# The queries of two attentions, made one batch earlier at two crossings between layers

## The chip, the cores and the metric

The kernel runs on one core of one Trainium2 chip. The metric is the device time of one execution in microseconds; the time given for a version is the median of its runs. "PE" is the engine for matrix products, "DVE", "ACT" and "POOL" are the vector, scalar and GpSimd engines, and "SP" is the engine whose queue issues most DMAs. Each engine works through its own queue in order.

## The reference

A decoder of four layers works on `x`, 8 batches of 256 tokens with 128 channels, and a context of 8 batches of 512 tokens. Each layer has a self-attention, a cross attention or the like, and a feed-forward part; each part reads a layer norm of `x` and is added to `x`:

```python
x = x + _L2_attn_ref(_layernorm(x, axis=-1), ...)            # sparse causal ("fenwick") attention
x = x + _L2_xattn_ref(_layernorm(x, axis=-1), ctx_1024, ...) # cross attention, 16 heads of 8
x = x + _L2_ffn_ref(_layernorm(x, axis=-1), ...)             # gate and up products, quantised to 8 bits
x = x + _L3_attn_ref(_layernorm(x, axis=-1), ...)            # causal attention, 16 heads of 8
```

Batches do not mix in the attentions. The L2 feed-forward part takes one maximum over all tokens for its quantisation scale, twice.

## The kernel before

`x` stays in on-chip memory as 16 tiles of 128 tokens, and `xt` holds the transposed layer norm of each batch, on which products work. A batch is "normed" once `_norm` (statistics on DVE, the power on POOL, `ln_z` on DVE) and `_normed` (two transposes on PE into `ln_ps`, one copy by ACT into `xt`) have run for it.

Work is written as Python generators that yield between steps, so that the steps of one layer can be put among those of the next. The framework turns the program into one instruction queue for each engine and may move an instruction ahead of others that it does not depend on; the products of the attentions are pinned to program order by `_Heads.mm` and `_Heads.turn_over`.

The attentions with 16 heads of 8 (the cross attention of layer 2 and the causal attention of layer 3 among them) share `_Heads`. For each batch, `steps(b)` makes keys, queries and values:

- `project("k", ...)` and `project("q", ...)`: one product on PE into `mh_kps` or `mh_qps`, an evacuation with bias by ACT into `mh_kf` or `mh_qf` (L426), and a split into two parts by POOL into `mh_kp` or `mh_qp` (L428 and L429);
- `spread_k` and `spread_q`: four and eight DMAs issued by SP (L434 and L439), which lay the heads out into `mh_k` and `mh_q`;
- `values`: products into `mh_vps`, copied by ACT into `mh_v`;
- `rest`: a row added to `x` by POOL (`pre_add`, the lines `x<-x,mh_row`).

`first()` does this for batch 0 in two halves with one yield between them: first keys, part of the spreading and the values, and then queries, `pre_add` and the rest of the spreading. Afterwards `_heads_attention` computes `mh_sps` (scores for the row maximum), and with a lag the exponentials and outputs. Its generator argument `guest` is work of the layer before it, for later batches, which goes on among the steps of the attention.

There are two crossings that matter here.

**From the sparse attention to the cross attention of layer 2**, in `_middle`. `fa(0, 1)` is the sparse attention of batches 0 and 1. It goes through half-batches `t` = 0 to 3 with `weigh` (products `fa_kvps` of shifted inputs, evacuated by DVE at L1115 and by ACT at L1118, then softmax, then weighted values on POOL at L1137 and L1139) and `apply` (`fa_o`, `fa_tps`, `fa_ot`, `fa_yps`, and at odd `t` the layer norm), and yields the number of a batch when that batch is normed. Before it runs, `next(begun)` has made the keys and values of batch 0. After it has run to its end, `next(begun, None)` makes the queries.

**From the feed-forward part of layer 2 to the causal attention of layer 3**, in `_l2_ffn`. `pair(0, ...)` takes the down products of batches 0 and 1 (`qf_hq`, `qf_dps`, `qf_y`), adds them to `x`, and then norms batch 0 and batch 1, with a yield of the batch number after each. When it is done, `E.draining()` runs the whole `beginning` of the causal attention: keys, values and queries of batch 0.

In the lines of the profile, L460 is the helper `_Heads.mm`, L463 is `_Heads.transpose`, and L215 is the copy into `xt`.

Of the kernel before, what the change touches and what calls it, by code (L numbers as in the profile page):

```python
# [187 lines left out]
def _norm(E, b, engine=None):  # L188

    nc = E.nc  # L190
    st = E.ln.tile([P, 2, 6], F32, name="ln_st")
    mv = E.ln.tile([P, 2, 2], F32, name="ln_mv")
    for q in range(2):
        nc.vector.bn_stats(st[:, q, :], E.x[:, 2 * b + q, :])
        nc.vector.bn_aggr(mv[:, q, :], st[:, q, :])  # L195
    rstd = E.ln.tile([P, 2], F32, name="ln_rstd")
    nc.gpsimd.tensor_scalar(rstd, mv[:, :, 1], EPS, None, ALU.add)  # L197
    nc.gpsimd.tensor_tensor(rstd, rstd, E.neg_half[:, :2], ALU.pow)  # L198
    z = E.ln.tile([P, 2, D], F32, name="ln_z")
    for q in range(2):  # L200
        (engine or nc.vector).tensor_scalar(  # L201
            z[:, q, :], E.x[:, 2 * b + q, :], mv[:, q, 0:1], rstd[:, q : q + 1], ALU.subtract, ALU.mult
        )
    return z


def _normed(E, b, z, psum, turn_over=None):

    ps = psum.tile([P, 2, D], F32, tag="g", name="ln_ps")
    for q in range(2):  # L210
        if turn_over:
            turn_over(ps[:, q, :], z[:, q, :])
        else:
            E.nc.tensor.transpose(ps[:, q, :], z[:, q, :], E.ident)
    E.nc.scalar.copy(E.xt(b), ps.rearrange("p q t -> p (q t)"))  # L215
# [6 lines left out]
def _run(steps):  # L222
    for _ in steps:
        pass
# [955 lines left out]
def plain_pe(E):  # L1180

    E.mm, E.transpose = E.nc.tensor.matmul, E.nc.tensor.transpose
    E.turn_over = lambda out, in_: E.nc.tensor.transpose(out, in_, E.ident)


def _middle(E, names, then):

    nc = E.nc  # L1190
    plain_pe(E)
    banks = lambda to, name, bufs, side="left": to.enter_context(
        E.tc.tile_pool(name=name, bufs=bufs, space=PSUM, side=side)
    )
    if names != MIDDLE:
        for n in names:
            with ExitStack() as scope:
                pg = E.mid_ln = banks(scope, "mid_pg", 6)
                E.banks = SimpleNamespace(fa=pg, rk=pg, ln=pg)
                unit = {  # L1200
                    "L0_ffn": _l0_ffn, "L1_attn": _l1_attn, "L1_xattn": _l1_xattn, "L1_ffn": _l1_ffn,
                    "L2_attn": _l2_attn,
                }[n](E, scope, *([pg] if n in MIDDLE[:3] else []))
                if n == "L2_attn":
                    _run(unit(0, 4))
                    continue
                for g in range(4):
                    _run(unit(g) or ())
        E.close_weights()
        return  # L1210
    last, psum, scope, early = (ExitStack() for _ in range(4))
    E.mid_ln = banks(psum, "mid_ln", 1)
    mid = banks(scope, "mid_pg", 4, "right")
    moe = _l0_ffn(E, scope, banks(early, "moe_pg", 3))
    ra, xa = _l1_attn(E, scope, mid), _l1_xattn(E, scope, mid)
    rk = _l1_ffn(E, scope, "right")
    E.banks = SimpleNamespace(rk=mid, ln=E.mid_ln)
    for s in range(4):
        if s > 2:
            _run(rk(s - 3))  # L1220
        if s > 1:
            xa(s - 2)
        if s:
            ra(s - 1)
        moe(s)
    early.close()
    E.close_big()
    ra(3)
    xa(2)
    xa(3)  # L1230
    scope.close()
    E.banks.fa = banks(psum, "fa_pg", 3)
    fa = _l2_attn(E, last)
    guest = then in HEADS
    begun = E.beginning(then)
    if guest:
        next(begun)
    _run(fa(0, 1))
    if guest:
        next(begun, None)  # L1240
    psum.close()

    def rest():
        if guest:
            g = E.heads.g
            E.mm, E.turn_over, E.transpose = E.heads.mm, E.heads.turn_over, E.heads.transpose
            E.banks = SimpleNamespace(fa=g, rk=g, ln=g)
        with ExitStack() as own:
            if not guest:
                g = banks(own, "mid_pg2", 6)  # L1250
                E.banks = SimpleNamespace(fa=g, rk=g, ln=g)
            yield from fa(1, 3, _l1_ffn(E, own))
        last.close()
        E.close_weights()
        if guest:
            yield from _l2_ffn_weights(E, E.heads.g)

    E.guest = rest()
    if not guest:
        _run(E.guest)  # L1260
# [5 lines left out]
def _quantise(E, pool, to, of, inv):  # L1266

    n, w = to.shape[0], to.shape[1]
    u = pool.tile([P, 512], F32, name="qf_t")[:n, :w]
    E.nc.vector.tensor_scalar(u, of, inv, 127.0, ALU.mult, ALU.min)  # L1270
    E.nc.vector.tensor_scalar(u, u, -128.0, ROUND, ALU.max, ALU.add)
    E.nc.scalar.activation(to, u, AF.Identity, bias=E.unround[:n, :])
# [53 lines left out]
def _l2_ffn(E, ctx):  # L1326
# [11 lines left out]
    wk = ctx.enter_context(E.tc.tile_pool(name="qf", bufs=2))  # L1338
    pg = ctx.enter_context(E.tc.tile_pool(name="qf_pg", bufs=6, space=PSUM))
# [47 lines left out]
    def pair(g, pool, bank):  # L1387

        hq = pool.tile([P, 3, 512], BF16, name="qf_hq")
        for c, n in QUARTERS:  # L1390
            _quantise(E, pool, hq[:n, c, :], h[:n, c, g, :], inv_h[:n, :])
            yield
        ps = bank.tile([P, 4, D], F32, tag="g", name="qf_dps")
        for t in range(4):
            for c, n in QUARTERS:
                E.mm(ps[:, t, :], hq[:n, c, t * P : t * P + P], f.down[:n, c, :], start=c == 0, stop=c == 2)
        y = pool.tile([P, 4, D], F32, name="qf_y")
        nc.vector.tensor_tensor(y, ps, f.row.unsqueeze(1).to_broadcast([P, 4, D]), ALU.mult)
        yield
        zs = []  # L1400
        for b in range(2):
            E.add(2 * g + b, y[:, 2 * b : 2 * b + 2, :])
            zs.append(_norm(E, 2 * g + b))
        for _ in range(3):
            yield
        for b in range(2):
            _normed(E, 2 * g + b, zs[b], bank, E.turn_over)
            yield 2 * g + b

    guest = E.following in HEADS  # L1410
    for g in range(1 if guest else 4):
        _run(pair(g, wk, pg))
    E.draining()

    def rest():
        E.mm, E.turn_over, E.transpose = E.heads.mm, E.heads.turn_over, E.heads.transpose
# [12 lines left out]
def _l3_ffn(E, ctx):  # L1429
# [103 lines left out]
}  # L1533
LAYERS = {
    "L2_xattn": _l2_xattn, "L2_ffn": _l2_ffn,
    "L3_attn": _l3_attn, "L3_xattn": _l3_xattn, "L3_ffn": _l3_ffn,
}
# [4 lines left out]
def kernel(ctx: ExitStack, tc: tile.TileContext, ins, at, out, layers=ALL):  # L1542
    nc = tc.nc
    const = ctx.enter_context(tc.tile_pool(name="const", bufs=1))
    E = SimpleNamespace(nc=nc, tc=tc, ins=ins)
# [88 lines left out]
    begun = set()  # L1634

    def heads():

        E.heads = _Heads(E, hd)
        E.unfilled = list(E.heads.fills())
# [3 lines left out]
    def beginning(layer):  # L1643

        if layer in HEADS and layer not in begun:
            begun.add(layer)
            if not E.heads:
                heads()
            fills, E.unfilled = E.unfilled, []
            for f in fills[:4]:  # L1650
                f()
            HEADS[layer](E)
            yield from E.heads.first()
            for f in fills[4:]:
                f()

    def begin(layer):

        for _ in beginning(layer):
            pass  # L1660
# [62 lines left out]
    for i, part in enumerate(parts):  # L1723
# [13 lines left out]
        if kind(layer) == "middle":  # L1737
            hd.close()
            E.heads = None
            prefetch(then)  # L1740
            _middle(E, part, following)
            continue
# [34 lines left out]
```

## Time and profile before

| | us |
|---|---|
| median of 3 runs | 1782.96 (1779.84 to 1785.97) |
| profiled execution, its time | 1784.95 |
| profiled execution, its span | 1783.2 |
| PE busy | 1471.9 (83%) |
| DVE busy | 1149.2 (64%) |
| ACT busy | 881.3 (49%) |
| POOL busy | 495.7 (28%) |
| mean granted PE clock | 0.921 |

The span runs from the first to the last instruction. The time also holds 1.75 us around it. PE is the busiest engine over the whole span, but the share is a mean over many layers, and both crossings lie in slices where it is lower. Where the text gives a point of time such as "906.29", it is in microseconds from the start of the span.

A line of a timeline reads: start, duration, engine, line of the kernel, operation, written tile `<-` read tiles, shapes and the count of merged instructions. What stands in square brackets is the idle time of the engine ahead of it and who ended that. Matrix products on 32-bit numbers appear as two records each.

### The profile page before, as it was taken

How to read it: one execution, taken by the hardware profiler on the slowest of the kernel's cores; microseconds unless marked ns; L12 is line 12 of the kernel's file. 1: busy time of each engine (PE TensorE's matmuls, PEld its weight loads, DVE VectorE, ACT ScalarE, POOL GpSimd, SP SyncE). 2: the span in 40 equal slices, each digit the busy share in tenths (PEclk: the TensorE clock that was granted, in tenths of full speed). 3: DMA queues.
4: the chain of work that ended last, by engine and by line, in shares of the span. 5: the costliest groups of instructions: out<-in, count | busy, mean ns of one | idle time of the engine just before them, and what ended most of it. 6: DMA issues, size and time to landing. Idle time of an engine off the chain costs nothing. (4 is left out here: it accounts for less than half of the span.)

```text
span 1783.2 us, 29345 instructions
## 1 busy us (share of the span) xinstructions
PE 1471.9 (83%) x10141; PEld 1064.4 (60%) x10141; DVE 1149.2 (64%) x3857; ACT 881.3 (49%) x1830; POOL 495.7 (28%) x987
## 2 busy tenths in 40 slices
PE   5689989998999998785558888878946799899986
PEld 3457677766665555453446656656624677677763
DVE  4567666764636676777657777767565666466756
ACT  7245455554652344325525656447643465455543
POOL 3122222221110121223423334332103433244422
PEclk9899999999999999997869999989965899899999
DMA  4011011104100000000111011111001221112100
GB/s 153 13 36 36 4 36 37 36 15 150 38 1 1 1 1 1 0 1 1 24 40 29 17 37 37 37 37 42 5 10 51 87 67 49 49 50 56 44 1 24
DMA packets 47236, 60.43 MB, mean 34 GB/s; under 512 B 5232, under 2 KB 36976, under 8 KB 46448
## 3 DMA queue, kind: packets, MB, share of 16 engines
q1 hardware_dynamic: 44720, 56.99, 11.8%
q8 instruction: 80, 1.31, 0.3%
q10 hardware_dynamic: 2368, 1.57, 0.3%
q14 instruction: 68, 0.56, 0.1%
HBM read 14.50 MB, written 1.05 MB: 9 GB/s over the span
## 5 line engine op out<-in xcount | busy, mean ns | idle before, releaser
L460 PE MATMUL mh_sps<-mh_k,mh_q 96*128 96x512 f32 (+2 forms) x1024 | 324.9, 400 | 51.0 <-DMA mh_q<-mh_qp 24.5
L460 PE MATMUL mh_bsps<-mh_q,mh_k 128*128 128x256 f32 (+1 forms) x1536 | 355.0, 337 | 8.5 <-DMA mh_q<-mh_m 4.4
L596 ACT ACTIVATE mh_e<-mh_bsps 128x512 f32<-128x512 f32 x512 | 281.2, 599 | 121.2 <-PE mh_bsps L460 114.2
L460 PEld LDWEIGHTS mh_bsps<-mh_q,mh_k 128*128 128x128 f32 x1536 | 267.9, 199 | 33.5 <-issue 6.9
L460 PEld LDWEIGHTS mh_sps<-mh_k,mh_q 96*128 96x128 f32 x1024 | 174.0, 204 | 98.6 <-issue 43.3
L523 DVE CUSTOM_DVE_ANT_0 mh_rest<-mh_sps,mask_b 128x512 bf16<-128x512 f32 x256 | 167.1, 684 | 86.7 <-PE mh_sps L460 83.7
L460 PE MATMUL mh_ops<-mh_e,mh_v 128*32 128x256 f32 (+1 forms) x3072 | 196.9, 377 | 1.3 <-DVE mh_nm L523 0.8
L542 DVE TENSOR_REDUCE mh_nm<-mh_sps 128x1 f32<-128x512 f32 x256 | 165.2, 681 | 34.4 <-PE mh_sps L460 34.0
L583 ACT ACTIVATE mh_e<-mh_bsps 128x384 f32<-128x384 f32 x256 | 118.7, 493 | 58.5 <-PE mh_bsps L460 35.0
L460 PEld LDWEIGHTS mh_ops<-mh_e,mh_v 128*32 128x32 f32 x3072 | 95.7, 113 | 67.7 <-issue 8.2
L197 POOL TENSOR_SCALAR ln_rstd<-ln_mv 128x2 f32<-128x2 f32 x96 | 22.0, 229 | 386.6 <-DVE ln_mv L195 386.3
L549 POOL CAST mh_hi<-mh_nm 128x8 fp32r<-128x8 f32 x128 | 25.0, 196 | 344.3 <-DVE mh_nm L523 208.5
L523 DVE CUSTOM_DVE_ANT_0 mh_rest<-mh_sps,causal 128x128 bf16<-128x128 f32 (+1 forms) x256 | 79.4, 352 | 49.1 <-PE mh_sps L460 47.0
L523 DVE CUSTOM_DVE_ANT_0 mh_rest<-mh_sps,km_q 128x128 bf16<-128x128 f32 (+1 forms) x256 | 79.4, 350 | 43.6 <-PE mh_sps L460 42.2
L460 PE MATMUL mh_bsps<-mask_t,ident 128*128 128x512 bf16 x256 | 99.9, 390 | 0.4 <-ACT mh_e L596 0.4
L561 ACT CAST mh_m<-mh_mps 8x256 fp32r<-8x256 f32 x128 | 46.1, 360 | 100.7 <-PE mh_mps L463 99.4
L215 ACT COPY xt<-ln_ps 128x256 f32<-128x256 f32 x96 | 36.0, 375 | 117.1 <-PE ln_ps L463 62.1
L629 ACT COPY mh_osb<-mh_ops 128x256 f32<-128x256 f32 x128 | 47.6, 372 | 86.3 <-PE mh_ops L460 86.1
L886 ACT ACTIVATE moe_si<-moe_gps 128x512 f32<-128x512 f32 x64 | 38.0, 597 | 104.9 <-PE moe_gps L884 81.3
L201 DVE TENSOR_SCALAR ln_z<-x,ln_mv,ln_rstd 128x128 f32<-128x128 f32 x136 | 43.4, 360 | 55.1 <-POOL ln_rstd L198 55.0
L895 PEld LDWEIGHTS moe_dps<-w_L_ffn,moe_act 128*128 128x128 f32 x512 | 66.2, 205 | 15.7 <-issue 8.0
L884 PE MATMUL moe_ups<-xt,w_L_ffn 128*128 128x512 f32 x128 | 69.7, 627 | 6.9 <-ACT moe_si L886 4.8
(360 smaller groups left out, 3081.1 us busy)
## 6 DMA issues: line engine op xcount, KB each, us to landing
mh_k<-mh_kp SPq DMA_DIRECT2D x64, 256.0 KB
mh_q<-mh_qp SPq DMA_DIRECT2D x256, 64.0 KB
mh_k<-mh_kp SPq DMA_DIRECT2D x64, 128.0 KB
w_L_ffn<-in_w_L_ffn SPq DMA_DIRECT2D x2, 1558.0 KB
w_L_attn<-in_w_L_attn SPq DMA_DIRECT2D x2, 1056.0 KB
ctx_t<-in_ctx_t SPq DMA_DIRECT2D x4, 512.0 KB
mh_q<-mh_m ACTq DMA_DIRECT2D x128, 8.0 KB
w_L_ffn<-in_w_L_ffn SPq DMA_DIRECT2D x2, 687.0 KB
```

Source lines behind the costliest of these rows:

```text
L201: (engine or nc.vector).tensor_scalar(z[:, q, :], E.x[:, 2 * b + q, :], mv[:, q, 0:1], rstd[:, q : q + 1], ALU.subtract, ALU.mult)
L215: E.nc.scalar.copy(E.xt(b), ps.rearrange("p q t -> p (q t)"))
L460: return self.E.tc.keep_in_program_order(self.E.nc.tensor.matmul(*a, **kw))
L523: nc.vector.tensor_tensor_reduce(rest[:, : scores.shape[1]], scores, lowered, -1.0, -FLOOR, ALU.add, ALU.min, accum_out=at)
L542: nc.vector.tensor_reduce(u.nm[:, c, col], ps, AX.X, ALU.max, negate=True)
L561: nc.scalar.copy(m, ps[:8].rearrange("p c q -> p (c q)"))
L583: nc.scalar.activation(e, ps, AF.Exp, scale=scale)
L596: nc.scalar.activation(e, ps, AF.Exp, scale=scale)
L629: nc.scalar.copy(osbs[b][:, u4 % 2, :], ops)
L884: nc.tensor.matmul(ps, W("w13")[:, o : o + P], xt, start=True, stop=True)
L886: nc.scalar.activation(si, pgate, AF.Silu)
L895: nc.tensor.matmul(ps[:, t, :], act[:, c, t * P : t * P + P], W("w2")[:, o : o + P], start=c == 0, stop=c == 1)
```

## The change

The cross attention's queries of batch 0 are now made when `fa` reports batch 0 as normed, while it still works on batch 1. A yield is added in `beginning`, after `first()`, so that the fills of the second buffer set stay behind the end of `fa`. In the feed-forward part, `E.draining()` is called between the norm of batch 0 and the norm of batch 1.

```diff
--- before.py
+++ after.py
@@ _middle
     begun = E.beginning(then)
     if guest:
         next(begun)
-    _run(fa(0, 1))
+    for b in fa(0, 1):
+
+        if guest and b == 0:
+            next(begun)
     if guest:
         next(begun, None)
     psum.close()
@@ _l2_ffn
     guest = E.following in HEADS
     for g in range(1 if guest else 4):
-        _run(pair(g, wk, pg))
-    E.draining()
+        for b in pair(g, wk, pg):
+            if guest and b == 0:
+                E.draining()
@@ beginning
             HEADS[layer](E)
             yield from E.heads.first()
+            yield
             for f in fills[4:]:
                 f()
```

The built instruction queues of the two versions differ as follows, and nowhere else. At the first crossing, PE's `mh_qps` moves from behind the transposes of batch 1's norm to the middle of the `fa_kvps` of the last half-batch (after the fifth of its nine offsets); ACT's `mh_qf` moves from behind batch 1's `xt` copy to between the second and the third of five `fa_v` copies; POOL's two `mh_qp` instructions move ahead of the last half-batch's `fa_v` (L1137), its norm and batch 1's `pre_add`. At the second crossing, PE's order `mh_kps`, `ln_ps` x2, `mh_vps`, `mh_qps` becomes `mh_kps`, `mh_vps`, `ln_ps`, `mh_qps`, `ln_ps`, and ACT's copy of batch 1 into `xt` moves behind `mh_qf`. The queues of DVE and SP are the same as before, and so is POOL's at the second crossing.

## The prediction

> **What bounds the kernel here.** I first took the waits between 880 and 930 us, where the cross attention begins, and between 1335 and 1360 us, where the causal attention begins. PE's longest waits on a transfer there are these two:
>
> ```profile
> PE mh_sps L460 <- DMA mh_q<-mh_qp: 7.5, 1, 7.5
> PE mh_sps L460 <- DMA mh_q<-mh_qp: 8.8, 1, 8.8
> ```
>
> The columns are microseconds in total, times, and the longest. At each crossing the first scores wait for the spreading of batch 0's queries. The timeline of the first crossing, engine by engine, shows what stands ahead of that spreading:
>
> ```profile
> 879.44 4.13 PE L1114 MATMUL fa_kvps<-w_L_attn,xt 128*128 128x256 f32 x12
> 897.21 0.73 PE L1183 MATMUL ln_ps<-ident,ln_z 128*128 128x128 f32 x2 [2.42 <-DVE ln_z L201]
> 897.74 1.06 PE L460 MATMUL mh_qps<-xt,w_L_xattn 128*128 128x256 f32 x2
> 906.29 2.34 PE L460 MATMUL mh_sps<-mh_k,mh_q 96*128 96x512 f32 x4 [7.49 <-DMA mh_q<-mh_qp]
> ...
> 879.68 0.37 ACT L215 COPY xt<-ln_ps 128x256 f32<-128x256 f32 x1 [2.64 <-PE ln_ps L1183]
> 897.98 0.37 ACT L215 COPY xt<-ln_ps 128x256 f32<-128x256 f32 x1 [4.03 <-PE ln_ps L1183]
> 898.84 0.47 ACT L426 ACTIVATE mh_qf<-mh_qps,w_L_xattn 128x256 f32<-128x256 f32 x1 [0.49 <-PE mh_qps L460]
> ...
> 888.10 2.18 POOL L1137 TENSOR_TENSOR fa_v<-fa_v,fa_sc 128x1152 f32<-128x1152 f32 x1 [8.17 <-DVE fa_sc L1135]
> 899.85 0.72 POOL L429 TENSOR_TENSOR mh_qp<-mh_qf,mh_qp 128x256 fp32r<-128x256 f32 x1
> ...
> 899.80 5.34 SPq L439 DMA_DIRECT2D mh_q<-mh_qp  x8
> ```
>
> Batch 0 is in `xt` at 880.05 (879.68 + 0.37), but its queries are only multiplied at 897.74, behind the norm of batch 1. From there the chain is `mh_qps`, `mh_qf`, `mh_qp`, eight DMA issues of 0.67 us each (5.34 / 8), landing 1.15 us after the last issue (906.29 - 905.14). DVE, ACT and POOL do nothing between 900.57 and 906.29: the whole core waits for this chain. What follows hangs on `mh_sps`: DVE's next work waits 9.68 us for it, ACT's 11.07 us for a product queued behind it on PE.
>
> **First crossing: when the queries are ready.** `mh_qps` now stands behind two products of the row at 879.44. Its 12 records in the half clock come 0.43 us apart (879.44, 879.87, 880.30 and on), so two products take it to 881.15, with `xt` of batch 0 there since 880.05. Two records end near 882.2; `mh_qf` takes 0.47 to 882.7; the two `mh_qp` instructions (0.40 and 0.72, with the 0.07 between them) end near 883.9, in POOL's idle 8.17 us, 4 us ahead of L1137; SP, idle since 870.9, issues from about 883.2 to 888.6, and the spreading lands near 889.8. That is 9 us ahead of its use, so the DMAs cost nothing on the path; if that cover were gone, each microsecond would come back as a wait of `mh_sps`.
>
> **First crossing: what it costs batch 1.** PE, ACT and POOL have the moved instructions ahead of batch 1's work. On PE it is 2 x 0.43 = 0.85 us in front of four `fa_kvps`; DVE's L1115 waits for these (1.28 and 0.51 us idle ahead of its last ones), so PE is on batch 1's path here. But the granted clock goes from half to full at about 882.2 (below), and two of the displaced records, which ran at 0.43 us, then run at 0.21: 0.43 us stays. ACT waits 1.33 and 0.56 us ahead of the copies behind `mh_qf`, which hides its 0.47. Bounds: 0 if L1115 sets the pace, 2.44 (0.85 + 0.47 + 0.40 + 0.72) if all stands in series. I take 0.43, by the rows of PE, since they are the ones waited for.
>
> **First crossing: what is late next.** Behind batch 1's transposes PE meets `mh_sps` at once. Its other waits are on ACT, whose last act for the sparse attention is the copy of batch 1 into `xt`, ended at 898.35; that reading frees the bank on which the attention's score tiles can lie. So `mh_sps` starts at 898.35 + 0.43 + 0.05 = 898.83 in place of 906.29: 7.46 us gained. The 0.05 is how long `mh_kps` at 1341.05 came after its copy (1340.62 + 0.37). If that copy isn't waited for, PE is free behind the transposes, at 897.94 + 0.43 = 898.37, and the gain is 7.9. Queues, buffers and instructions behind that point are the same, and every engine is idle before it, so the rest moves as a block. The loss bound gives 906.29 - 898.40 - 2.44 = 5.4.
>
> **Second crossing.** Here the timeline of POOL and SP says something else than the diff:
>
> ```profile
> 1342.74 0.90 POOL L1623 TENSOR_TENSOR x<-x,mh_row 128x256 f32<-128x256 f32 x1 [0.72 <-DVE ln_z L201]
> 1343.59 0.58 POOL L428 CAST mh_kp<-mh_kf 128x256 fp32r<-128x256 f32 x1
> 1345.98 0.78 POOL L429 TENSOR_TENSOR mh_qp<-mh_qf,mh_qp 128x256 fp32r<-128x256 f32 x1
> ...
> 1344.20 2.66 SPq L434 DMA_DIRECT2D mh_k<-mh_kp  x4
> 1347.03 5.34 SPq L439 DMA_DIRECT2D mh_q<-mh_qp  x8
> ```
>
> POOL's queue isn't changed: `mh_kp` stays behind the row at 1342.74, which waits for `ln_z` of batch 1. So the keys' spreading still starts at 1344.20 and holds SP until 1346.86; the queries' spreading, now at 1347.03, can start 0.17 us earlier and no more. `mh_qps` moves from 1343.84 to about 1343.1, `mh_qf` by 0.38 (to 1344.6, behind a `qf_hq`), `mh_qp` with it to an end near 1346.3, all hidden behind SP's four issues. Gain 0.17, bounds 0 and 0.38. Batch 1's `xt` copy moves back by about 1.8 us; its first reader, `mh_kps` of batch 1, runs at 1354.68, so 9 us cover it.
>
> **Sum.** 7.46 + 0.17 = 7.6 us. The profiled execution, 1784.95 us around a span of 1783.2, would take 1777.3. It lies 2.0 above the median of 1782.96, which becomes 1775.3.
>
> **The clock.** The windows of one microsecond show the granted clock change:
>
> ```profile
> 882.00:883.00 1.00, 1.00 (x6) 0.90 (x5) 0.42 (x1) 0.30 (x1) 0.00 (x0) 0.89 0.00 0
> 889.00:890.00 1.00, 0.00 (x0) 0.00 (x0) 0.00 (x0) 0.00 (x0) 1.00 (x1) 0.52 0.03 8
> 912.00:913.00 1.00, 1.00 (x6) 1.00 (x5) 0.15 (x2) 0.99 (x2) 0.00 (x0) 0.53 0.00 0
> ```
>
> The third number from the right is the clock. Between 0.5 and 1.0 it switched at 882.22, 889.04 and 912.94: gaps of 6.82 and 23.90 us, 2 and 7 times 3.41. On that grid the next edges after a start at 898.83 are 899.3 and 902.7. In before, full clock came 6.65 us after `mh_sps` began (906.29); with the edge at 902.7 it would come 3.9 us after. The Trainium skill, "TensorE: Matmul & The Clock Gate", section "What's actually happening", says that the clock is freed after a busy window of about 3.4 us, falls back after an idle one, and that the windows run free of the kernel's start; by that rule the gain would be the one of the second rival below, and in an execution with another phase anything down to the plain sum. The grid of 3.41 agrees with it; that the phase varies no run here shows.
>
> **Rivals.** (1) The forecast, 7.6 gained, 1775.3: chance 0.62. For it: the idle engines before 906.29 and the unchanged queues behind. (2) The earlier edge also shortens the start: DVE idles 1.23 and 0.84 us there waiting for PE, but ACT's row `rk_r` ends at 913.55 behind a table load that PE does not speed up, against 914.81 for its reader, so at most 1.26 of it: 8.9 gained, 1774.1, chance 0.16. (3) The moved instructions cost batch 1 all they take, 2.44: 5.4 gained or a little less with the second crossing at nothing, 1777.6, within the bound below; chance 0.18. Against it: the idle of ACT and POOL there. (4) Slower: the spreading, now between 883 and 890, runs beside batch 1's softmax and POOL's L1137, and contention for the on-chip memory stretches that chain. It runs 15.2 us, from 883.2 to 898.4, and must lose more than 7.6 + 5.35 = 12.95 us to end slower, that is run 1.85 times as long; at that point the time is 1788.3, at twice as long 1790.6. Against it: the keys' spreading at 867.69 to 870.90 ran beside an L1115 of 0.42 and an L1124 of 1.22 us, and without a transfer beside them they took 0.42 and 1.35 (for 1152 elements in place of 1024). Chance 0.04. That the change does nothing is excluded for the first crossing by the order of the queues, and is nearly the forecast for the second.
>
> **Numbers.** About 0.3% (5.35 us) is what a measurement of this kernel can tell from no change; faster means below 1777.6. Cases 1 and 2 lie below, but the three runs span 6 us, so that a gain of 7.6 can measure as less than 5.35; I move 0.02 of theirs over. Faster 0.76, same 0.20, slower 0.04. The range goes from 1771.0 (case 2 less 3 us of spread) to 1780.0 (case 3 with 2.4 of spread).
>
> **What would show it.** In the profile after, `mh_qps` should stand inside the `fa_kvps` near 881, SP's eight issues should lie near 883 to 889, and the first `mh_sps` should wait for ACT's copy, not for a DMA, about 0.5 us behind it. At the second crossing SP's row `x4` and the wait of `mh_sps` on the DMA should stay, shorter by 0.2. The forecast is wrong if `mh_sps` starts later than 901 on this scale, if L1137 starts over 1 us later than 888.1, or if the cross attention's stretch from its first `mh_sps` to the first `mh_sps` of the causal attention (447.4 us, 906.29 to 1353.69) grows by over 2 us.

## The result, and the profile after

| | before | after |
|---|---|---|
| median, us | 1782.2 (1779.84 to 1785.97, 6 runs) | 1772.33 (1771.43 to 1777.3, 6 runs) |
| profiled execution, its time | 1784.95 | 1771.95 |
| profiled execution, its span | 1783.2 | 1770.2 |
| mean granted PE clock | 0.921 | 0.928 |

The changed kernel takes 0.9949 of the time of the kernel before, 95% interval 0.9934 to 0.9964: it is faster, by 6.4 to 11.8 us. The predicted gain was 7.6. (A ratio compares the runs made side by side and need not be the quotient of the two medians to the last digit.)

PE's waits now, around the first crossing and then around the second, have these two lines in place of the first pair that the prediction showed:

```profile
PE mh_sps L460 <- ACT xt L215: 0.5, 1, 0.5
PE mh_sps L460 <- DMA mh_q<-mh_qp: 9.3, 1, 9.3
```

At the first crossing no wait on the spreading is left. At the second the wait is still there. The timeline of the first crossing (PE, ACT, POOL, SP) shows the new order:

```profile
874.55 1.06 PE L460 MATMUL mh_qps<-xt,w_L_xattn 128*128 128x256 f32 x2
892.00 0.73 PE L1183 MATMUL ln_ps<-ident,ln_z 128*128 128x128 f32 x2 [2.43 <-DVE ln_z L201]
893.19 2.37 PE L460 MATMUL mh_sps<-mh_k,mh_q 96*128 96x512 f32 x4 [0.46 <-ACT xt L215]
...
873.39 0.37 ACT L215 COPY xt<-ln_ps 128x256 f32<-128x256 f32 x1 [2.50 <-PE ln_ps L1183]
892.77 0.37 ACT L215 COPY xt<-ln_ps 128x256 f32<-128x256 f32 x1 [4.04 <-PE ln_ps L1183]
...
876.67 0.72 POOL L429 TENSOR_TENSOR mh_qp<-mh_qf,mh_qp 128x256 fp32r<-128x256 f32 x1
882.87 2.18 POOL L1137 TENSOR_TENSOR fa_v<-fa_v,fa_sc 128x1152 f32<-128x1152 f32 x1 [5.48 <-DVE fa_sc L1135]
...
876.61 5.34 SPq L439 DMA_DIRECT2D mh_q<-mh_qp  x8
```

Two executions don't reach this place at the same time, so I count from ACT's copy of batch 0 into `xt`, at 873.39 here and 879.68 before. SP issues from 3.22 to 8.56 behind it, where before it issued from 20.12. The first `mh_sps` comes 19.80 behind it, where before it came 26.61: 6.81 us gained in this pair. It starts 0.05 behind the end of the copy of batch 1 (892.77 + 0.37).

The two profiled executions differ by 13.0 us, more than the change explains. The difference splits at three points into 6.29 ahead of the copy at 873.39, where the instruction queues are the same; 6.81 at the first crossing; 2.23 from the first `mh_sps` to that of the causal attention (447.40 before, 445.17 after); and -2.33 behind it (429.51 and 431.84). The 2.23 need not be the change's: e2_second_only below, without the change at the first crossing, has 444.77 there.

### The profile page after: what moved, and what is told of

Its sections match the earlier page's. It is cut to its first block, busy times and chain, and to the rows that moved or that the text cites. A ratio compares the mean times of both kernels' runs of the same rounds, so it can differ in the third digit from the quotient of the medians.

```text
span 1770.2 us, 29308 instructions
## 1 busy us (share of the span) xinstructions
PE 1462.7 (83%) x10103; PEld 1055.3 (60%) x10141; DVE 1148.5 (65%) x3857; ACT 881.5 (50%) x1830; POOL 495.7 (28%) x987
## 5 line engine op out<-in xcount | busy, mean ns | idle before, releaser
L460 PE MATMUL mh_bsps<-mask_t,ident 128*128 128x512 bf16 x219 | 84.7, 387 | 0.4 <-ACT mh_e L596 0.4
L463 PE MATMUL mh_mps<-ident,mh_nx 128*8 128x128 f32 x256 | 51.1, 282 | 27.7 <-POOL mh_nx L552 23.2
```

Source lines behind the costliest of these rows:

```text
L460: return self.E.tc.keep_in_program_order(self.E.nc.tensor.matmul(*a, **kw))
L463: return self.E.tc.keep_in_program_order(self.E.nc.tensor.transpose(*a))
```

## The experiments

**One crossing at a time.** The first run has only the first and third hunk of the change, the second only the second hunk.

```diff
# e1_first_only: before, and
-    _run(fa(0, 1))
+    for b in fa(0, 1):
+        if guest and b == 0:
+            next(begun)
...
             yield from E.heads.first()
+            yield
# e2_second_only: before, and
-        _run(pair(g, wk, pg))
-    E.draining()
+        for b in pair(g, wk, pg):
+            if guest and b == 0:
+                E.draining()
```

> Only the first crossing of the change (queries of the cross attention while batch 1 is still worked on). Theory A, all of the gain is the spreading of the first crossing that is now hidden: first mh_sps about 6.8 us earlier after the xt copy of batch 0 (19.8 us in place of 26.6), and the time like the changed kernel's within 2 us, 1771 to 1775. Rival B, the second crossing brings the 2 to 3 us by which the gain went over the forecast: 1774.5 to 1777 here. In both the second crossing's stretch from the xt copy of batch 0 to the first mh_sps stays at 13.1 us.

> Only the second crossing of the change (causal attention begun between the norms of batch 0 and batch 1). Theory A: the time of before within 1.5 us, 1781 to 1784, and 13.0 to 13.2 us from the xt copy of batch 0 to the first mh_sps, since SP's four issues for the keys hold the eight for the queries. Rival B: 2 to 3 us less than before, 1779 to 1780.

The kernel before ran at 1781.14 us beside them (median of 23 runs, 1776.52 to 1786.41). The first crossing alone took 1772.32 (1770.27 to 1774.35), ratio 0.9951 (0.9938 to 0.9964); the second alone 1780.38 (1776.2 to 1782.57), ratio 0.9996 (0.9987 to 1.0005). The whole effect that these runs can tell is that of the first crossing.

Why the second brings nothing is seen in the timeline of the changed kernel there (POOL, SP, PE):

```profile
1328.23 0.58 POOL L428 CAST mh_kp<-mh_kf 128x256 fp32r<-128x256 f32 x1
1330.24 0.78 POOL L429 TENSOR_TENSOR mh_qp<-mh_qf,mh_qp 128x256 fp32r<-128x256 f32 x1
...
1328.84 2.66 SPq L434 DMA_DIRECT2D mh_k<-mh_kp  x4
1331.66 5.34 SPq L439 DMA_DIRECT2D mh_q<-mh_qp  x8
1338.36 1.19 PE L460 MATMUL mh_sps<-mh_k,mh_q 96*128 96x128 f32 x4 [9.31 <-DMA mh_q<-mh_qp]
```

`mh_qp` is now complete at 1331.02, 0.48 us ahead of the end of the key issues (1331.50); before it was 0.10 ahead (1346.76 and 1346.86). Still the query issues begin 2.82 us behind the start of the keys' issues, as before (1347.03 - 1344.20 = 2.83). From the copy of batch 0 into `xt` to `mh_sps` it is 13.10 us, before 13.07.

**The same queries later.** If the gain is the time by which the spreading comes ahead of its use, it must shrink with a later request. Two runs ask for the queries eight and seven steps of `fa` behind batch 0.

```diff
# after, and (written shorter here; since is None ahead of the loop)
-        if guest and b == 0:
+        since = 0 if b == 0 else since if since is None else since + 1
+        if guest and since == 8:      # e4_late;  7 in e4_mid
             next(begun)
```

> Changed kernel, but the cross attention's queries are asked for in the last half-batch's apply: mh_qps stands behind the fa_tps of that half (about 13 us later), ahead of fa_yps and of batch 1's norm. If the spreading is what counts, it lands about 4 us behind batch 1's xt copy, mh_sps waits for the DMA again (3 to 4 us), and only 3 to 4.5 us of the first crossing's 6.8 are gained: 1775 to 1779. If the gain came from something else than the spreading's cover (less work behind batch 1's norm, say), mh_sps follows the xt copy as in the changed kernel and the time is 1771 to 1775.

> Changed kernel, but the queries are asked for one step later: mh_qps behind the fa_kvps, mh_qf behind the last fa_v, both in idle time, POOL's mh_qp still ahead of L1137. Theory: the cost on batch 1's chain (xt copy of batch 0 to xt copy of batch 1: 18.3 us before, 19.4 in the changed kernel) is PE's two records among the fa_kvps, so it goes back to 18.3 to 18.6 and mh_sps begins 18.7 to 19.1 us after the first copy, 0.7 to 1.1 us earlier than in the changed kernel. Rival, the cost is contention of the spreading with batch 1's softmax: it stays at 19.2 or more, since the spreading now lies fully beside it.

In the timeline of e4_late the wait on the spreading is back, at half its size:

```profile
893.45 1.06 PE L460 MATMUL mh_qps<-xt,w_L_xattn 128*128 128x256 f32 x2
902.07 2.35 PE L460 MATMUL mh_sps<-mh_k,mh_q 96*128 96x512 f32 x4 [3.62 <-DMA mh_q<-mh_qp]
...
895.51 5.34 SPq L439 DMA_DIRECT2D mh_q<-mh_qp  x8
```

`mh_sps` comes 22.35 us behind the copy of batch 0 (879.72), a gain of 4.26 (26.61 - 22.35). The time was 1775.67 (1773.69 to 1781.65), ratio 0.9975 (0.9963 to 0.9987), which is 4.5 us. Gain and wait go together.

In e4_mid the products of the queries stand behind all of the half-batch's `fa_kvps`, and POOL's part is still ahead of L1137. Its timeline (PE, POOL, DVE):

```profile
877.77 0.60 PE L460 MATMUL mh_qps<-xt,w_L_xattn 128*128 128x256 f32 x2
893.05 2.37 PE L460 MATMUL mh_sps<-mh_k,mh_q 96*128 96x512 f32 x4 [0.46 <-ACT xt L215]
...
879.52 0.72 POOL L429 TENSOR_TENSOR mh_qp<-mh_qf,mh_qp 128x256 fp32r<-128x256 f32 x1
882.74 2.18 POOL L1137 TENSOR_TENSOR fa_v<-fa_v,fa_sc 128x1152 f32<-128x1152 f32 x1 [2.49 <-DVE fa_sc L1135]
...
879.66 0.75 DVE L1125 TENSOR_TENSOR fa_sc<-fa_sc,fa_sb 128x144 f32<-128x144 f32 x1
```

From the copy of batch 0 (873.96) to that of batch 1 it is 18.67 us, in e1_first_only 19.02 and before 18.30; to `mh_sps` it is 19.09, a gain of 7.52, where e1_first_only has 7.16 (26.61 - 19.45). The spreading (879.47 to 884.81) lies right beside the softmax and the start of L1137, which still took 2.18 us. The time was 1770.15 (1769.19 to 1772.0, 5 runs), ratio 0.9942 (0.993 to 0.9954). This is the lowest ratio of the runs with the queries alone moved, but its interval overlaps with those of the changed kernel and of e1_first_only; that it is faster than these is shown for the crossing only, by 0.36 us against e1_first_only. The interval, 8.2 to 12.5 us, lies above the 7.52 that the crossing shows; where the rest comes from, this execution doesn't show.

**The changed kernel again.** The median of the first measurement lay 9.9 us below the kernel before, more than the crossing shows.

> The changed kernel again, beside the runs of before of the same call. If its gain is the 6.8 to 7.3 us that the first crossing's stretch shows in every trace, the ratio is 0.995 to 0.9965; if something more comes of the change elsewhere, it is 0.9945 or lower again, and the stretches behind the first crossing differ from those of before by over 2 us in the same direction as in the first profile.

It took 1772.75 us (1770.33 to 1780.63) beside 1782.17 of the kernel before (29 runs, 1776.1 to 1791.58): ratio 0.9959 (0.9944 to 0.9975), 7.3 us. The medians alone lie 9.4 us apart here, so they overstate the gain. The crossing has the same numbers as in the first profile: copy to copy 19.37, to `mh_sps` 19.80. A gain of 7.2 us, a ratio of 0.9960, lies in the intervals of this run, of the first measurement and of e1_first_only, so none of them asks for a second effect; the intervals don't exclude one of 2 us either.

**The second crossing's true limit.** If SP's twelve issues bind there, ACT's queue can take four of them.

```diff
# e3_split_causal: after, and in spread_q
+            issuer = nc.scalar if r and self.layer in ("L3_attn",) and b == 0 else nc.sync
-            nc.sync.dma_start(...)
+            issuer.dma_start(...)
# e3_split_both: the same on e4_mid, with ("L0_xattn", "L3_attn")
```

> Changed kernel, and four of the eight DMAs that spread the causal attention's first queries are issued by ACT in place of SP. If the second crossing is held by SP's issues (four for the keys, eight for the queries, 0.67 us each), the last issue comes 2.6 us earlier and the stretch from batch 0's xt copy to the first mh_sps falls from 13.1 to 10.3 to 10.8 us; the time falls by 2 to 3 us against the changed kernel. If the transfers themselves hold it (DMA busy 0.45, 122 GB/s in that stretch), it stays at 12.5 or more.

> The version with the queries one step later (e4_mid), with the same split between SP and ACT for the causal attention and for the first cross attention of the kernel, where mh_sps also waits for its first spreading (7.6 us at about 62 us). Theory of SP's issues: 2.4 us less at each place, 4 to 5.5 us under e4_mid, 1764.5 to 1767. Rival: at the first place ACT has the sparse work's copies queued behind its four issues (2.5 us), which then come late for the linear attention, and nothing is gained there: 1767 to 1769.

The timeline of e3_split_causal:

```profile
1336.31 2.82 ACTq L440 DMA_DIRECT2D mh_q<-mh_qp  x4
1334.96 2.66 SPq L434 DMA_DIRECT2D mh_k<-mh_kp  x4
1337.85 3.65 SPq L440 DMA_DIRECT2D mh_q<-mh_qp  x4
1343.34 1.19 PE L461 MATMUL mh_sps<-mh_k,mh_q 96*128 96x128 f32 x4 [8.19 <-DMA mh_q<-mh_qp]
```

SP's four issues span 3.65 us, where four took 2.67 in the changed kernel. The issues themselves are no slower: the first took 0.64 us (1337.85 to 1338.49) and the last three 2.01 (from 1339.49). Between them SP stood for 1.00 us, and its waits name the releaser, a landing of this same spreading:

```profile
SPq L440 <- DMA mh_q<-mh_qp: 1.0, 1, 1.0
```

The changed kernel has no such wait here; why the second issue needs that landing isn't settled. Besides, the data came 1.84 us behind the last issue (1343.34 - 1341.50), in the changed kernel 1.36. So of 2.67 us of issues taken off SP only 1.14 are seen between copy and `mh_sps` (11.96 for 13.10), which lies between the two expectations, and none in the time: 1774.23 (1769.5 to 1778.25), ratio 0.9953 (0.9936 to 0.997), beside 1772.75 of the changed kernel. The second run took 1770.51 (1768.31 to 1773.07), ratio 0.9939 (0.9919 to 0.9958), no different from e4_mid's and above both of its expectations. Its trace has about 1 us at each place and not 2.4: 11.99 for 13.06 from copy to `mh_sps` at the second crossing, and 8.26 for 9.20 at the first cross attention. SP's issues do bind the stretch, since it became shorter, but what the split gains is less than these runs can tell. The Trainium skill, "DMA: Bandwidth & Descriptors", section "Issuing engines are not separate DMA queues", says that issuing from several engines saves only the sequencer's time; the direction agrees, and here not half of that time was saved.

**Past the last copy.** With the spreading hidden, `mh_sps` waits for batch 1's norm. This run begins the cross attention without it: the last part of batch 1's sparse attention becomes guest work of the cross attention. No step is left out.

```diff
# e8_guest: after, with the split of e3_split_causal, and
+    begin_fa, since = fa(0, 1), None
+    for b in begin_fa:
+        # queries at b == 0 as in after; since counts the steps behind it
+        if guest and since == 7:
+            break
...
+            yield from begin_fa
             yield from fa(1, 3, _l1_ffn(E, own))
...
-    _heads_attention(E, ctx, guest=guest, known=(0, 1), pace=lambda t: 1.25)
+    _heads_attention(E, ctx, guest=guest, known=(0,), pace=lambda t: 2.0 if t < 7 else 1.25)
```

> Changed kernel with the split for the causal attention, and the end of batch 1's sparse attention (from the second fa_yps of its first half on) made a guest of the cross attention: mh_sps of the first head stands ahead of it on PE. If batch 1's norm is what is late next, mh_sps begins when the spreading has landed, about 10 to 10.5 us after batch 0's xt copy in place of 19.8, and some of the idle time of PE, DVE and POOL ahead of batch 1's norm is filled: 2 to 6 us less than the split version alone. Rival: only the first heads move, the chain of batches 2 and 3 behind it (rk and its norms) still waits for batch 1's work, and the time is that of the split version within 1 us, or longer by what the interleaved steps wait for each other.

It took 1784.97 us (1782.7 to 1787.17), ratio 1.0014 (1.0002 to 1.0026): slower than the kernel before, though the attention began early. One line of its timeline, and two of its waits from the first `mh_sps` to that of the causal attention:

```profile
887.27 1.19 PE L461 MATMUL mh_sps<-mh_k,mh_q 96*128 96x512 f32 x2 [5.75 <-DMA mh_q<-mh_qp]
...
DVE mh_nm L543 <- PE mh_sps L461: 34.7, 30, 3.6
ACT fa_v L1119 <- DVE fa_pr L1116: 32.9, 16, 5.5
```

and the same two waits of e0_again:

```profile
DVE mh_nm L542 <- PE mh_sps L460: 25.0, 28, 2.2
ACT fa_v L1118 <- DVE fa_pr L1115: 25.7, 11, 7.0
```

`mh_sps` came 10.16 us behind the copy of batch 0 (877.11), again waiting on the spreading. But from that copy to the causal `mh_sps` it took 476.6 us, in e0_again 464.9 (19.80 + 445.06). The 9.6 us won at the start were lost, and 11.8 more. The loss lies inside the attention: its last output copy (ACT's `mh_osb`) comes 420.3 us behind the copy of batch 0 (1297.42 - 877.11), in e0_again 407.4 (1281.18 - 873.82). The two waits agree with steps that wait longer for each other, though a sum of waits doesn't show which of them cost time. The order of the guest's steps and their pace changed together, so which of the two costs more stays open.

## Why the prediction was right, point by point

**The mechanism held.** `mh_qps` stands 1.16 us behind the copy of batch 0; SP's issues lie at 3.22 to 8.56 behind it, predicted 3.5 to 8.9; and `mh_sps` waits for ACT's copy of batch 1 and no more for a DMA, with the 0.05 us that the sum had. The stretch to the causal attention didn't grow (445.17 and 445.06, before 447.40). That e4_late gives back part of both the wait and the time shows the cause, not only the order. The time of 1772.33 lies 3.0 us below the 1775.3 that was forecast. The crossings don't explain these 3 us: in the traces they give 7.2, less than the 7.6 of the sum. The repeated measurement, 7.3 us, agrees with the traces.

**The term that was too small: the cost on batch 1's chain.** The sum had 0.43 us; copy to copy it grew by 1.08 (18.30 to 19.38) in the profiled pair, and this is why the first crossing gave 6.81 there and not 7.46. DVE's rows show where. First the reduction and the last softmax step of before, then the same of after:

```profile
883.94 1.35 DVE L1124 TENSOR_REDUCE fa_sc<-fa_pr 128x144 f32<-128x1152 f32 x1
887.64 0.31 DVE L1135 TENSOR_TENSOR fa_sc<-fa_sc,fa_red 128x144 f32<-128x144 f32 x1
```

```profile
878.42 1.35 DVE L1124 TENSOR_REDUCE fa_sc<-fa_pr 128x144 f32<-128x1152 f32 x1
882.13 0.31 DVE L1135 TENSOR_TENSOR fa_sc<-fa_sc,fa_red 128x144 f32<-128x144 f32 x1
```

Behind the copy of batch 0, L1124 starts at 4.26 before and at 5.03 after, 0.77 us later. The prediction's 0.43 for PE supposed that the clock goes full 2.54 behind the copy, as in before. In this execution it went full near 876.94, 3.55 behind it (the third number from the right is the clock):

```profile
876.00:877.00 1.00, 1.00 (x4) 0.82 (x3) 0.43 (x1) 0.16 (x2) 0.73 (x2) 0.53 0.00 0
```

Executions at the same phase of the clock separate the two. e1_first_only, with the same queues here, went full at 2.54 like before: L1124 starts at 4.68, 0.42 later than before, so PE's term was right. e2_second_only, with the queues of before here, went full at 3.45: L1124 starts at 4.61, so 0.35 is the phase alone. Paired by phase, copy to copy grows by 0.72 both times (18.30 to 19.02; 18.66 to 19.38), and the first crossing gives 7.16 (26.61 to 19.45) and 7.18 (26.98 to 19.80), where the sum had 7.46.

What the sum lacked is thus 0.29 us, and it is POOL's: L1137 starts 0.43 us behind the end of L1135, before 0.15. It does so in each version with `mh_qps` among the `fa_kvps`; what holds it isn't settled. The sum's bounds, 0 and 2.44, held. The mark for L1137 didn't: it was to start at most 1 us late, and 9.48 behind the copy against 8.42 is 1.06 late. The mark was meant as a sign of contention and left no room for the phase of the clock.

**Contention with the transfer (rival 4) falls.** In e4_mid the spreading lies closer to the softmax and to L1137 than in the changed kernel, and batch 1's chain is shorter there, 18.67 us for 19.02 in e1_first_only at the same phase. In the changed kernel DVE's L1125 ran beside the spreading (876.61 to 881.95) and took no longer than before:

```profile
879.89 0.30 DVE L1125 TENSOR_TENSOR fa_sc<-fa_sc,fa_sb 128x144 f32<-128x144 f32 x1
```

So the cost there follows the place of the products in PE's queue, not the transfer. But e4_mid's chain is still 0.37 us longer than before's (18.67 for 18.30, at the same phase), and this is not PE's: L1124 starts 4.23 us behind the copy, before 4.26. What grew is L1125, 0.75 us in place of 0.30, and what ran beside it there is POOL's second `mh_qp` instruction (see the last section). The moved work still collides with batch 1's softmax, through POOL.

**The earlier clock edge (rival 2) is the execution's, not the change's.** From the first `mh_sps` to the `ln_ps` behind it the time went from 12.84 to 11.86 us, with full clock 4.2 us behind the start. But e2_second_only, without the change at this crossing, has 11.63, and e3_split_causal, with it, 12.86. That agrees with the clock rule that the prediction cites from the Trainium skill: the phase varies between executions, and about 1 us of this start goes with it, here with the 0.35 us above against it.

**The second crossing** had 0.17 in the sum, with 0 as its lower bound, and gave nothing. The prediction read the 0.17 between the last key issue and the first query issue as a wait for `mh_qp`. The prediction's own rows speak against that: `mh_qp` was complete at 1346.76 (1345.98 + 0.78), 0.10 us ahead of the end of the last key issue. The gap stays at 0.16 with `mh_qp` complete 0.48 ahead of that end, so it is no wait for `mh_qp`; what fills it isn't shown.

## What to carry to other kernels

Where a whole core idles for one short chain ahead of a new stage, look for the earliest point at which its input exists, and move the chain there; it pays until the next wait, here batch 1's norm, 7 us on. Put the moved products behind the ones that another engine waits for, not among them: e4_mid did so, and batch 1's copy came 0.35 us sooner than in e1_first_only. And a request made earlier in the program moves nothing if the queue that carries it still holds earlier work: read that queue at the crossing first.

## What the runs showed of the hardware that was not expected

- In e4_mid DVE's L1125, an addition of two operands in on-chip memory, took 0.75 us with POOL's `mh_qp` (879.52 to 880.24) running beside it; before it took 0.30, without. In e3_split_both, with the same order, it again took 0.75. The Trainium skill, "SBUF — State Buffer", section "SBUF: two separate sides", says that a DVE operation with two inputs in this memory contends with a GpSimd (POOL) one that reads it, since the second input comes through a read interface that the two share, and that transfers don't contend with engines. Both rows agree, as do, for the transfers, the changed kernel's L1125 of 0.30 us and e4_mid's L1137 of 2.18 us with the spreading beside them.
- With the spreading split over the queues of SP and ACT, SP waited 1.0 us for a landing in the middle of its issues, in e3_split_causal, e3_split_both and e8_guest alike; in before and after it issues all twelve at the second crossing without such a wait. The issues themselves stay at 0.67 us each.
- With the same queues up to there, the copy of batch 0 began anywhere from 873.39 to 879.72 us in the profiles of before, after, e0_again, e1_first_only, e2_second_only, e4_late and e4_mid. That is nearly the size of the effect, so the change had to be read from stretches between fixed points and not from spans.
